# Macaron block with an S4 layer in the middle: waves of the quantized feed-forward regrouped, the last pair of a wave deferred, and a convolution with 28 block products

## The chip, the cores and the metric

The kernel runs on one core of one Trainium2 chip. The metric is the time of one execution on the device in microseconds (us). The engines are TensorE (PE, its weight loads listed apart as PEld), VectorE (DVE), ScalarE (ACT), GpSimd (POOL) and SyncE (SP), which here only issues transfers.

## The reference, cut to what matters

The input has 2 x 1024 rows of 1024 elements. Three stages are added to it, each on a layer norm of the running `x`:

```python
x = L0_attn_u                                      # (2, 1024, 1024)
x = x + 0.5 * ffn(layernorm(x))
x = x + s4(layernorm(x))
x = x + 0.5 * ffn(layernorm(x))                    # the same weights again

def ffn(x):                                        # 4-bit weights, groups of 128 rows
    Wg, Wu, Wd = (dequant(w) for w in (gate, up, down))   # (w4 - (z4 + 1)) * scale[group]
    return (silu(x @ Wg) * (x @ Wu)) @ Wd          # 1024 -> 2752 -> 1024

def s4(u):                                         # along the last axis, length L = 1024
    K = ifft(at_roots(Lambda, p, q, B, Ct, step)).real
    y = irfft(rfft(u, 2 * L) * rfft(K, 2 * L))[..., :L]   # a causal convolution with K
    return y + D * u
```

## The kernel before, in words

**Jobs.** The 2048 rows are cut into four blocks `b` of 512 rows (`TB`), of four tiles `t` of 128. A job `(b, k)` is one feed-forward on one block, first (`k` = 1) or second (`k` = 3). Eight jobs run in the order `(0,1) (1,1) (0,3) (1,3) (2,1) (3,1) (2,3) (3,3)`, here jobs 0 to 7. Each is `gate_up` and then `down`.

**gate_up.** The 2752 columns of gate and of up are 21 chunks `f` of 128 and a half chunk of 64. A *pair* is the gate and the up unit of one chunk; the half chunk's gate and up share one unit of 128. Each unit holds one of PSUM's eight banks as an accumulator `pg` (128 x 512). `WAVES` groups pairs into waves: five of three pairs, two of two, and one of two pairs and the half chunk. A wave has eight *steps*, one for each group of 128 input rows; `STEPS` has 64. A step multiplies every unit twice: with `hi` and `lo`, two parts of the transposed and normalized input (`xTh`, float32r; `xTl`, float16). The order in a step: the first half of the units with `lo`, then with `hi`; the other units with `hi`, then with `lo`. A unit's place in that list is its *position*: 0 is the first pair's gate, 1 its up, and so on.

**Rescales.** Quantized weights stay integers. After each group but the last, `scaled` multiplies the accumulator in place with the ratio of one group's scale to the next (L539 on ScalarE, L541 on VectorE); gate units go to ScalarE, up units to VectorE, and in job 0 position 1 also to ScalarE.

**gated.** When a pair has its eighth group, ScalarE makes `g` with Silu (L597), VectorE `hf` = up x `g` (L600), and GpSimd splits it into `hh` and `hl` (L602, L604). `hf` has two buffers (`hfpool`), `g` three. `gated_half` (L608 on) does the same for the half chunk with VectorE in GpSimd's place. Then `give_back` frees the pair's banks. `bank` hands out the bank that was handed out or given back longest ago and isn't held.

**down.** 2 x 22 steps: a half `a` of the output columns and a chunk `f`; four accumulators `po`, two matmuls each a step (`hl`, `hh`), rescaled in the same way.

**Weights.** `wq` and `wdq` are scratch in HBM with the integers as float32. Job 0 makes them while it runs (`first_weights`): the packed words are fetched, split into bytes (`split`), and `dequantize` subtracts the zero points on VectorE (L454 `q`, L486 `qd`) and writes to `wq` (L458) or `wdq` (L488) on SP. For wave `w` that is at steps 8w-12 to 8w-5; down's 48 pieces begin 12 steps before the end of `gate_up`, one a step, and go on in `down`. `load_w` (L523) and `load_down` (L531) read weights four steps ahead (`AHEAD`). Loads and dequantized tiles share one ring of buffers, `w` (`wpool`, 8).

**Hooks.** Other work is hung on steps by `at(up, step, ...)` for `gate_up` and `at(dn, step, ...)` for `down`; a hook is written ahead of its step's matmuls. After a first feed-forward the next job's `gate_up` carries the S4 stage of the previous block: `moments` and `deviations` (statistics), then for each of four tiles `norm` (VectorE), two steps on `swap` (`turn_whole`: eight transposes, a copy on ScalarE and one on VectorE), two steps on `conv`; then `moments` again and `save`, which writes the block to HBM. That is jobs 1, 2, 5 and 6. In jobs 2, 5 and 6 tile `t` has its `norm` at step 8 + 4t; in job 1 all is 30 steps later, since steps 2 on carry `s4_tables`, which makes the convolution kernel K (`s4_response`) and its Toeplitz matrix (`s4_toeplitz`) once. In jobs 3 and 4, step 44 has the statistics of the next block; in job 2 step 30 has a check of the group indices (`in_order`, `ps_ok`).

**convolve.** A tile's 1024 positions are eight blocks `c` of 128. The Toeplitz matrix has one 128 x 128 block per distance `d` (`blocks[:, d]`). The first four output blocks are ten block products (L915), the last four use sums and differences (`sums`, `after`, `ahead`), 21 blocks in 13 products (L934). In float32 the profile has two matmuls for each product. Three VectorE adds of 512 columns bring the results into `x` (L923, L950, L953).

**Order.** The calls above give the text an order, but a scheduler in the framework puts each engine's instructions into its queue; `in_order_of_writing` ties them to the text where it is used. Tiles of a pool get buffers from a ring by tag, and an instruction that needs a buffer waits until the last user is done.

Of the kernel before, what the change touches and what calls it, by code (L numbers as in the profile page):

```python
# [12 lines left out]
I32 = mybir.dt.int32  # L13
# [21 lines left out]
HALF = INTER - WIDE * P  # L35
WAVES = [list(range(3 * w, 3 * w + 3)) for w in range(5)] + [[15, 16], [17, 18], [19, 20]]
STEPS = [(w, g) for w in range(len(WAVES)) for g in range(GK)]
# [15 lines left out]
def macaron_s4_kernel(  # L53
# [40 lines left out]
    hpool = ctx.enter_context(tc.tile_pool(name="h", bufs=2 * NF))  # L94
    wpool = ctx.enter_context(tc.tile_pool(name="w", bufs=8))
    gpool = ctx.enter_context(tc.tile_pool(name="g", bufs=3))
# [28 lines left out]
    def t4(name):  # L125
        return xpool.tile([P, HID], F32, tag="x", name=name)
# [416 lines left out]
    def gate_up(j, b, hooks):  # L543
        hi, lo = pieces[b]
        ps = {}
        ready = {s: load_w(j, s) for s in range(AHEAD)}
        for s, (wi, g) in enumerate(STEPS):
# [15 lines left out]
            for k, pos, done in turns:  # L563
# [18 lines left out]
                if g < GK - 1:  # L582
                    on_act = unit % 2 == 0 or (j == 0 and pos == 1)
                    if unit == 2 * WIDE:
                        on_act = g % 2 == 0
                    scaled(on_act, p, p, rat[:, unit, g : g + 1])
                elif unit == 2 * WIDE:
                    gated_half(j, ps[unit])
                    give_back(ps.pop(unit))
                elif unit % 2:  # L590
                    gated(j, unit // 2, ps[unit - 1], ps[unit])
                    give_back(ps.pop(unit - 1), ps.pop(unit))
        pieces.pop(b)

    def gated(j, f, pg, pu):
        g = gpool.tile([P, TB], F32, tag="g", name=f"g_{j}_{f}")
        nc.scalar.activation(g, pg, AF.Silu, scale=rat[:, 2 * f, GK - 1 :])  # L597
        hf = hfpool.tile([P, TB], F32, tag="hf", name=f"hf_{j}_{f}")
        last = rat[:, 2 * f + 1, GK - 1 :]
        nc.vector.scalar_tensor_tensor(hf, pu, last, g, ALU.mult, ALU.mult)  # L600
        hi = hpool.tile([P, TB], F32R, tag="h", name=f"hh_{j}_{f}")
        nc.gpsimd.tensor_copy(hi, hf)  # L602
        lo = hpool.tile([P, TB], F32R, tag="h", name=f"hl_{j}_{f}")
        nc.gpsimd.tensor_tensor(lo, hf, hi.bitcast(F32), ALU.subtract)  # L604
        h[f] = (hi, lo)

# [57 lines left out]

    toeplitz = const.tile([P, HID], F32, tag="toeplitz", name="toeplitz")

    blocks = toeplitz.rearrange("p (d m) -> p d m", d=NC)
    after = const.tile([P, 3, P], F32, tag="after", name="after")
    ahead = const.tile([P, 3, P], F32, tag="ahead", name="ahead")
    k_dram = dpool.tile([1, P - 1 + HID], F32, tag="k", name="k_dram")  # L670
# [175 lines left out]
    def s4_response():  # L846

        tables = [t4("s4_tc"), t4("s4_ts")]
        for i in range(2):
            nc.sync.dma_start(tables[i], c_dft[:, i, :])  # L850
        ps = bank("s4_k")
        for r in range(8):
            for i in range(2):
                nc.tensor.matmul(  # L854
                    ps[:, r : r + 1],
                    tables[i].rearrange("p (a r) -> p r a", r=8)[:, r, :],
                    s4["se"][:, i, r : r + 1],
                    start=(i == 0),
                    stop=(i == 1),
                )  # L860
        k = t4("s4_response")
        d, none = k[:1, 8:9], k[:1, P : 2 * P - 1]
        nc.sync.dma_start(d, dskip.unsqueeze(0))
        nc.gpsimd.memset(none, 0.0)
        nc.vector.tensor_scalar(k[:, :8], ps[:, :8], 1.0 / HID, None, ALU.mult)
        nc.vector.tensor_tensor(k[:1, 0:1], k[:1, 0:1], d, ALU.add)
        nc.sync.dma_start(k_dram[:, : P - 1], none)
        nc.sync.dma_start(k_dram[0, P - 1 :].rearrange("(a r) -> a r", r=8), k[:, :8])
        s4.clear()

    def s4_toeplitz():

        both = [t4("s4_rows"), t4("s4_turn")]
        rows, turn = both[0], both[1][:, :P]
        nc.gpsimd.memset(turn, 0.0)
        nc.gpsimd.affine_select(
            out=turn,
            in_=turn,
            pattern=[[1, P]],
            compare_op=ALU.not_equal,  # L880
            fill=1.0,
            base=1 - P,
            channel_multiplier=1,
        )
        first = k_dram[:]
        nc.sync.dma_start(rows, bass.AP(first.tensor, first.offset, [[1, P], [1, HID]]))
        for i in range(NH):
            ps = bank(f"s4_t{i}")
            nc.tensor.matmul(ps, turn, rows[:, bass.ts(i, 512)], start=True, stop=True)
            dst = toeplitz[:, bass.ts(i, 512)]  # L890
            if i:
                nc.vector.tensor_copy(dst, ps)
            else:
                nc.scalar.copy(dst, ps)
        for dst, d in ((after, 3), (ahead, 1)):
            nc.vector.tensor_tensor(dst, blocks[:, d : d + 5 : 2], blocks[:, 2:7:2], ALU.subtract)

# [10 lines left out]
    def convolve(b, t, s, name):  # L908
# [3 lines left out]

        ps = bank(f"pc_{name}_0")
        for c in range(4):
            nc.tensor.matmul(  # L915
                ps[:, P * c :],
                s[:, c, :],
                toeplitz[:, : 512 - P * c],
                start=(c == 0),
                stop=(c == 3),  # L920
            )
        part = x[b][t][:, :512]
        nc.vector.tensor_tensor(part, part, ps, ALU.add)  # L923

        sums = ypool.tile([P, TB], F32, tag="y", name=f"sums_{name}")
        sums = sums[:, : 3 * P].rearrange("p (c t) -> p c t", c=3)
        nc.gpsimd.tensor_tensor(sums, s[:, 0:6:2, :], s[:, 1:6:2, :], ALU.add)
        own = bank(f"pc_{name}_1")
        both = bank(f"pc_{name}_2")[:, : 2 * P].rearrange("p (y m) -> p y m", y=2)
        flat = own.rearrange("p (y m) -> p y m", y=4)  # L930
        upper, lower = flat[:, 0:4:2], flat[:, 1:4:2]

        def product(dst, lhsT, rhs, start=False, stop=False):
            nc.tensor.matmul(dst, lhsT, rhs, start=start, stop=stop, skip_group_check=True)  # L934

        for y in range(2):
            product(flat[:, 2 * y : 2 * y + 2], s[:, 4 + 2 * y, :], blocks[:, 0:2], start=(y == 0))
        for y in range(2):
            product(flat[:, 2 * y + 1], s[:, 5 + 2 * y, :], blocks[:, 0])
        for i in range(3):  # L940
            y = slice(max(0, i - 1), 2)
            d = slice(max(0, 1 - i), 3 - i)
            product(lower[:, y], s[:, 2 * i, :], after[:, d])
            product(upper[:, y], s[:, 2 * i + 1, :], ahead[:, d], stop=(i == 2))
        for i in range(3):
            y = slice(max(0, i - 1), 2)
            d = slice(2 * max(1, 2 - i), 2 * (3 - i) + 1, 2)
            product(both[:, y], sums[:, i, :], blocks[:, d], start=(i == 0), stop=(i == 2))
        part = x[b][t][:, 512:]
        nc.vector.tensor_tensor(part, part, own, ALU.add)  # L950
        part = part.rearrange("p (y h m) -> p y h m", y=2, h=2)
        twice = both.unsqueeze(2).to_broadcast([P, 2, 2, P])
        nc.vector.tensor_tensor(part, part, twice, ALU.add)  # L953

# [14 lines left out]
    def general():  # L969
# [22 lines left out]
        def gather_table(dst, s_dram, z_dram, groups, n, name):  # L992
# [4 lines left out]
            for k in range(3):  # L997
                nc.sync.dma_start(s[32 * k : 32 * k + groups, :], s_dram)
            z = small.tile([P, P], I32, tag="z", name=f"z_{name}")[96:P, : n // 8]
            nc.gpsimd.memset(z, 0)  # L1000
# [162 lines left out]
        for b in range(TOK // TB):  # L1163
# [4 lines left out]
            for t in range(NT):  # L1168
                s = turn_whole(normalized(b, t), f"gt_{b}_{t}")
                convolve(b, t, s, f"g{b}_{t}")  # L1170
            feed_forward(b, 3)
# [9 lines left out]
    def fast():  # L1181
        for j, (b, k) in enumerate(JOBS):
# [7 lines left out]
            if prev:  # L1190
# [3 lines left out]
                if pk == 1:  # L1194
                    late = 30 if j == 1 else 0
                    at(up, 4, lambda: moments(pb, 2))
# [6 lines left out]
                    def swap(t):  # L1203
                        s4x[t] = turn_whole(s4n.pop(t), f"st_{pb}_{t}")

                    def conv(t):
                        convolve(pb, t, s4x.pop(t), f"{pb}_{t}")

                    for t in range(NT):
                        at(up, late + 8 + 4 * t, lambda t=t: norm(t))  # L1210
                        at(up, late + 10 + 4 * t, lambda t=t: swap(t))
                        at(up, late + 12 + 4 * t, lambda t=t: conv(t))
                    at(up, late + 27, lambda: moments(pb, 3))
                    at(up, late + 28, lambda: deviations(pb, 3, LIFT))

# [3 lines left out]

                    at(up, late + 28, save)  # L1220
                else:
# [196 lines left out]
```

## Time and profile before

| | us |
|---|---|
| median of 3 runs | 2207.82 (2206.94 to 2211.19) |
| the profiled execution's own time | 2209.4 |
| its span, first to last instruction | 2207.6 |
| TensorE busy | 2114.3 (96%) |
| VectorE busy | 1702.9 (77%) |
| ScalarE busy | 1428.7 (65%) |
| GpSimd busy | 368.1 (17%) |

The mean granted TensorE clock is 0.989 of full speed. A group of instructions is read as: line, engine, operation, what it writes from what it reads, shape, count, busy time, mean duration in ns, then the idle time before it and what ended most of it. A wait is read as: the waiting engine and line, what it waited for, us in total, times, longest. In the timeline a row has start and length in us, engine, line, tiles and count, and in brackets the idle time ahead of it. Durations of matmuls overlap, so TensorE's pace is read from starts.

### The profile page before, as it was taken

The page shows a single profiled execution, that of the slowest core. Times are in us where ns is not written, and L with a number is a line of the kernel's source. Part 1 is how long each engine was busy: PE and PEld are TensorE (multiplying, and loading weights), DVE is VectorE, ACT ScalarE, POOL GpSimd, SP SyncE. Part 2 cuts the span into 40 slices and gives each one's busy share as a digit, 9 for nine tenths or more (in the row PEclk, how much of TensorE's full clock was granted, in tenths as well). Part 3 has the DMA queues.
Part 4 walks back from the last instruction along what each step waited for, and adds up shares of the span by engine and source line. Part 5 has one row for each costly group of instructions (what it writes and reads, how often), then busy time and mean ns, then how long its engine had stood idle before and what let it go on. Part 6 is the DMA issues. An engine that isn't in the chain of part 4 may idle for free.

```text
span 2207.6 us, 28034 instructions
## 1 busy us (share of the span) xinstructions
PE 2114.3 (96%) x9524; PEld 1420.1 (64%) x9524; DVE 1702.9 (77%) x2803; ACT 1428.7 (65%) x2245; POOL 368.1 (17%) x389
## 2 busy tenths in 40 slices
PE   5888889999999999999999999999999999999998
PEld 3444565566877658755686558776587765865576
DVE  7777969777786877777877787867778677777776
ACT  5667777555764577666766667646676467766665
POOL 0223301222011230122102220112201122012310
PEclk9999999999999999999999999999999999999999
DMA  7768775434453545644655454534455354564443
GB/s 249 248 225 271 242 255 165 140 108 157 134 158 115 171 135 155 193 145 119 208 163 174 127 172 134 158 115 153 138 137 154 115 177 136 155 194 146 133 131 119
DMA packets 163669, 359.93 MB, mean 163 GB/s; under 512 B 22395, under 2 KB 27572, under 8 KB 163518
## 3 DMA queue, kind: packets, MB, share of 16 engines
q1 hardware_dynamic: 162670, 356.50, 52.1%
q8 instruction: 78, 1.28, 0.2%
q10 hardware_dynamic: 592, 1.16, 0.1%
q0 software_dynamic: 256, 0.39, 0.1%
q14 instruction: 73, 0.60, 0.1%
HBM read 306.86 MB, written 50.73 MB: 162 GB/s over the span
## 4 chain that ended last, share of the span: by engine, by line
PE 73%; issue 7%; DVE 5%; POOL 2%; ACT 1%; DVEq 0%; POOLq 0%; ACTq 0%
PE pg L572 42%; PE po L636 24%; PE pc L934 3%; PE pc L915 1%; POOL hl L604 1%; DVE pg L541 1%; PE pb L658 1%; PE pt L215 1%; DVE hf L600 1%; DVE po L541 1%; POOL hh L602 1%; PE st L215 1%; DVE qd L486 0%; PE s_k L854 0%; ACT g L597 0%
## 5 line engine op out<-in xcount | busy, mean ns | idle before, releaser
L539 ACT ACTIVATE pg<-pg,rat 128x512 f32<-128x512 f32 x1264 | 799.9, 661 | 489.3 <-PE pg L572 487.5
L541 DVE TENSOR_TENSOR pg<-pg,rat 128x512 f32<-128x512 f32 x1144 | 761.5, 694 | 180.9 <-PE pg L572 176.1
L572 PE MATMUL pg<-xTh,w 128*128 128x512 f32 x2752 | 874.2, 444 | 12.4 <-DVE pg L541 9.9
L572 PE MATMUL pg<-xTl,w 128*128 128x512 f16 x2752 | 737.8, 384 | 32.7 <-DVE pg L541 14.5
L572 PEld LDWEIGHTS pg<-xTh,w 128*128 128x128 f32 x2752 | 522.4, 190 | 192.6 <-DVE pg L541 24.3
L636 PE MATMUL po<-hl,wd 128*128 128x512 f32 x1344 | 540.5, 403 | 15.7 <-DMA wd<-wdq 7.5
L539 ACT ACTIVATE po<-po,ratd 128x512 f32<-128x512 f32 x670 | 438.1, 662 | 162.5 <-PE po L636 161.8
L636 PE MATMUL po<-hh,wd 128*128 128x512 f32 x1344 | 525.3, 392 | 0.0
L541 DVE TENSOR_TENSOR po<-po,ratd 128x512 f32<-128x512 f32 x610 | 420.9, 698 | 99.2 <-PE po L636 95.4
L572 PEld LDWEIGHTS <-w 128*128 128x128 bf16 x2752 | 227.8, 99 | 370.4 <-issue 186.1
L602 POOL CAST hh<-hf 128x512 fp32r<-128x512 f32 x168 | 109.4, 651 | 1530.7 <-DVE hf L600 976.1
L636 PEld LDWEIGHTS po<-hl,wd 128*128 128x128 f32 x1344 | 253.0, 188 | 92.1 <-DVE po L541 19.7
L636 PEld LDWEIGHTS po<-hh,wd 128*128 128x128 f32 x1344 | 253.6, 189 | 46.3
L604 POOL TENSOR_TENSOR hl<-hf,hh 128x512 fp32r<-128x512 f32 x168 | 222.9, 1327 | 13.4
L600 DVE SCALAR_TENSOR_TENSOR hf<-pg,rat,g 128x512 f32<-128x512 f32 x168 | 124.3, 749 | 90.6 <-ACT g L597 42.8
L597 ACT ACTIVATE g<-pg,rat 128x512 f32<-128x512 f32 x168 | 110.8, 687 | 48.7 <-PE pg L572 38.5
L178 DVE BATCH_NORM_STATS2 stats<-x 128x6 f32<-128x512 f32 x96 | 63.6, 677 | 1.1
L215 PE MATMUL pt<-ident,xn 128*128 128x128 f32 x256 | 42.6, 283 | 11.0 <-ACT xn L1286 11.0
L238 DVE TENSOR_TENSOR xTl<-pt,xTh 128x512 f16<-128x512 f32 x56 | 38.4, 690 | 14.2 <-ACT xTh L237 13.4
L660 DVE TENSOR_TENSOR x<-x,pb 128x512 f32<-128x512 f32 x64 | 43.2, 679 | 6.2 <-PE pb L658 6.0
L215 PEld LDWEIGHTS pt<-ident,xn 128*128 128x128 f32 x256 | 33.1, 145 | 21.8 <-ACT xn L1286 12.8
L237 ACT CAST xTh<-pt 128x512 fp32r<-128x512 f32 x56 | 33.0, 590 | 18.8 <-PE pt L215 18.6
(151 smaller groups left out, 816.9 us busy)
## 6 DMA issues: line engine op xcount, KB each, us to landing
w<-wq SPq DMA_DIRECT2D x319, 384.0 KB
wd<-wdq SPq DMA_DIRECT2D x336, 256.0 KB
w<-wq SPq DMA_DIRECT2D x128, 256.0 KB
w<-wq SPq DMA_DIRECT2D x64, 320.0 KB
x<-in_L_attn_u_dram SPq DMA_DIRECT2D x30, 512.0 KB
wq<-q SPq DMA_DIRECT2D x40, 384.0 KB
wdq<-qd SPq DMA_DIRECT2D x32, 256.0 KB
xs<-x SPq DMA_DIRECT2D x16, 512.0 KB
```

The lines of the kernel that those rows point to most:

```text
L178: nc.vector.bn_stats(stats[:, t, i, :], x[b][t][:, bass.ts(i, 512)])
L215: nc.tensor.transpose(ps[:, bass.ts(k, P)], n[:, bass.ts(k, P)], ident)
L539: nc.scalar.activation(dst, src, AF.Copy, scale=sc)
L541: nc.vector.tensor_tensor(dst, src, sc.to_broadcast([P, TB]), ALU.mult)
L572: nc.tensor.matmul(p, weights, (lo, hi)[k][:, g, :], start=(g == 0 and not done), stop=(g == GK - 1 and done), skip_group_check=True,)
L597: nc.scalar.activation(g, pg, AF.Silu, scale=rat[:, 2 * f, GK - 1 :])
L600: nc.vector.scalar_tensor_tensor(hf, pu, last, g, ALU.mult, ALU.mult)
L602: nc.gpsimd.tensor_copy(hi, hf)
L604: nc.gpsimd.tensor_tensor(lo, hf, hi.bitcast(F32), ALU.subtract)
L636: nc.tensor.matmul(ps[c], w[:, bass.ts(c, P)], part, start=(f == 0 and k == 0), stop=(f == NF - 1), skip_group_check=True,)
L660: nc.vector.tensor_tensor(part, part, ps, ALU.add)
L934: nc.tensor.matmul(dst, lhsT, rhs, start=start, stop=stop, skip_group_check=True)
```

## The change

`WAVES` becomes seven waves of three pairs; the half chunk joins the last one, which then has seven units and holds seven banks. `STEPS` has 56. The ring `w` gets 7 buffers, as wide as the new last wave (896 columns).

`gated` issues Silu at once and returns the rest (`hf`, `hh`, `hl`, `give_back`). For all pairs but a wave's last it is called immediately; the last pair's is called in the next wave's first step behind the rescale of position 1, or at the end of `gate_up`.

`convolve` is a generator with two parts, first and last four output blocks, the second one step later; it makes 28 blocks in 24 products, with more sums on GpSimd and five VectorE adds (512, 256 and three of 512 columns). Its hooks stand at `norm` 8 + 4t in jobs 2, 5 and 6, and 33 + 3t in job 1; the statistics after them come one step earlier in 2, 5 and 6, nine steps earlier in job 1.

`s4_response` computes K in one row and not in 8 columns on 128 partitions; `s4_toeplitz` keeps only the blocks and differences that are used.

```diff
-WAVES = [list(range(3 * w, 3 * w + 3)) for w in range(5)] + [[15, 16], [17, 18], [19, 20]]
+WAVES = [list(range(3 * w, 3 * w + 3)) for w in range(7)]
-    wpool = ctx.enter_context(tc.tile_pool(name="w", bufs=8))
+    wpool = ctx.enter_context(tc.tile_pool(name="w", bufs=7))
@@ def gate_up
+        waiting = []
+        def finish():
+            while waiting:
+                waiting.pop()()
...
                     scaled(on_act, p, p, rat[:, unit, g : g + 1])
+                    if pos == 1:
+                        finish()
...
-                    gated(j, unit // 2, ps[unit - 1], ps[unit])
-                    give_back(ps.pop(unit - 1), ps.pop(unit))
+                    rest = gated(j, unit // 2, ps.pop(unit - 1), ps.pop(unit))
+                    if unit // 2 == fs[-1]:
+                        waiting.append(rest)
+                    else:
+                        rest()
+        finish()
@@ def gated
         nc.scalar.activation(g, pg, AF.Silu, scale=rat[:, 2 * f, GK - 1 :])
+        def rest():
...
+            give_back(pg, pu)
+        return rest
@@ def s4_response
-        for r in range(8):
-            for i in range(2):
-                nc.tensor.matmul(ps[:, r : r + 1],
-                    tables[i].rearrange("p (a r) -> p r a", r=8)[:, r, :], s4["se"][:, i, r : r + 1], ...)
-        nc.vector.tensor_scalar(k[:, :8], ps[:, :8], 1.0 / HID, None, ALU.mult)
+        for half in range(2):
+            for r in range(4):
+                for i in range(2):
+                    nc.tensor.matmul(ps[:1, bass.ts(r, P)], s4["se"][:, i, 4 * half + r : 4 * half + r + 1],
+                        tables[i].rearrange("p (a r) -> p r a", r=8)[:, 4 * half + r, :], ...)
+            nc.vector.tensor_scalar(k[:1]..., ps[:1]..., 1.0 / HID, None, ALU.mult)
@@ def s4_toeplitz
+        nc.vector.tensor_copy(near[:, 0:3], blocks[:, 0:3])
+        nc.vector.tensor_copy(near[:, 3], blocks[:, 4])
         for dst, d in ((after, 3), (ahead, 1)):
-            nc.vector.tensor_tensor(dst, blocks[:, d : d + 5 : 2], blocks[:, 2:7:2], ALU.subtract)
+            own = dst[:, 0:3]
+            nc.vector.tensor_tensor(own, blocks[:, d : d + 5 : 2], blocks[:, 2:7:2], ALU.subtract)
+            nc.vector.tensor_tensor(dst[:, 3], dst[:, 2], dst[:, 1], ALU.subtract)
+            nc.vector.tensor_tensor(dst[:, 2], dst[:, 0], dst[:, 1], ALU.subtract)
+        for i in range(2):
+            nc.vector.tensor_tensor(middle[:, i], blocks[:, 2 + 4 * i], blocks[:, 4], ALU.subtract)
@@ def convolve, the new body
+        nc.gpsimd.tensor_tensor(sums[:, 0:3], s[:, 0:6:2, :], s[:, 1:6:2, :], ALU.add)
+        nc.gpsimd.tensor_tensor(quad, s[:, 0:2, :], s[:, 2:4, :], ALU.add)
+        nc.gpsimd.tensor_tensor(sums[:, 3], sums[:, 0], sums[:, 1], ALU.add)
+        for o in range(2):
+            if o:
+                yield
+            own = bank(f"pc_{name}_{o}")
+            flat = own.rearrange("p (d m) -> p d m", d=4)
+            mine = s[:, 4 * o : 4 * o + 4]
+            product(flat[:, 0:2], mine[:, 0], near[:, 0:2], start=True)
+            product(flat[:, 1], mine[:, 1], near[:, 0])
+            product(flat[:, 2:4], mine[:, 2], near[:, 0:2])
+            product(flat[:, 3], mine[:, 3], near[:, 0])
+            product(flat[:, 3], mine[:, 0], after[:, 0])
+            product(flat[:, 2], mine[:, 1], ahead[:, 0], stop=(o == 0))
+            both = bank(f"pb_{name}_{o}")
+            if o == 0:
+                product(both[:, :P], sums[:, 0], near[:, 2], start=True, stop=True)
+            else:
+                for y in range(2):
+                    product(flat[:, 2 * y + 1], s[:, 2 - 2 * y], after[:, 2 + y])
+                    product(flat[:, 2 * y], s[:, 3 - 2 * y], ahead[:, 2 + y], stop=(y == 1))
+                twice = both.rearrange("p (y m) -> p y m", y=4)
+                product(twice[:, 0], sums[:, 1], middle[:, 0], start=True)
+                product(twice[:, 1], sums[:, 0], middle[:, 1])
+                product(twice[:, 1], sums[:, 2], near[:, 2])
+                for y in range(2):
+                    product(twice[:, y], sums[:, 3], near[:, 3])
+                product(twice[:, 3], quad[:, 0], after[:, 1])
+                product(twice[:, 2], quad[:, 1], ahead[:, 1], stop=True)
...
@@ def fast, the S4 hooks
-                    late = 30 if j == 1 else 0
+                    o, gap = (33, 3) if j == 1 else (8, 4)
...
-                        at(up, late + 8 + 4 * t, lambda t=t: norm(t))
-                        at(up, late + 10 + 4 * t, lambda t=t: swap(t))
-                        at(up, late + 12 + 4 * t, lambda t=t: conv(t))
-                    at(up, late + 27, lambda: moments(pb, 3))
-                    at(up, late + 28, lambda: deviations(pb, 3, LIFT))
+                        s = o + gap * t
+                        at(up, s, lambda t=t: norm(t))
+                        at(up, s + 2, lambda t=t: swap(t))
+                        at(up, s + 4, lambda t=t: conv(t))
+                        at(up, s + 5, lambda t=t: next(parts[t], None))
+                    done = o + 3 * gap + 6
+                    at(up, done, lambda: moments(pb, 3))
+                    at(up, done + 1, lambda: deviations(pb, 3, LIFT))
...
```

## The prediction

> **What bounds the kernel now.** I read the page, then the chain of waits, VectorE's waits and its timeline at a wave boundary, then windows on the narrow waves of job 0.
>
> ```profile
> PE 2114.3 (96%) x9524; PEld 1420.1 (64%) x9524; DVE 1702.9 (77%) x2803; ACT 1428.7 (65%) x2245; POOL 368.1 (17%) x389
> ...
> 933.34 0.69 DVE pg L541
> 934.04 0.04 issue
> 934.08 21.32 PE pg L572 x94
> ...
> 955.41 0.70 DVE pg L541
> 956.11 0.04 issue
> 956.15 21.32 PE pg L572 x94
> ```
>
> TensorE is the bound: 96% busy, and the chain runs along it. It leaves it at one repeating place: a wave of three pairs is 21.3 us of matmuls, then a VectorE rescale of 0.7 us. TensorE's timeline shows a step of 12 matmuls every 2.695 us inside a wave (0.2246 us each), so eight steps want 21.56 us; waves come 22.05 us apart. Each boundary loses 0.49 us. VectorE's waits and timeline say why:
>
> ```profile
> DVE hf L600 <- POOL hl L604: 33.9, 29, 1.4
> ...
> 951.90 1.52 DVE L600 SCALAR_TENSOR_TENSOR hf<-pg,rat,g 128x512 f32<-128x512 f32 x2 [0.79 <-ACT g L597]
> 954.74 0.75 DVE L600 SCALAR_TENSOR_TENSOR hf<-pg,rat,g 128x512 f32<-128x512 f32 x1 [1.32 <-POOL hl L604]
> 955.41 2.53 DVE L541 TENSOR_TENSOR pg<-pg,rat 128x512 f32<-128x512 f32 x4
> ```
>
> The third pair's `hf` needs one of two `hf` buffers and waits 1.32 us for GpSimd (`hh` and `hl`, 0.61 + 1.30 us a pair). The next wave's first VectorE rescale is ready at about 954.0 and stands behind it until 955.41.
>
> A second loss is in the narrow waves 5 to 7 (208 matmuls, 46.7 us at the wide pace). By the timeline they take 48.4 us in jobs 2, 5, 6, 7, about 50.8 in jobs 3 and 4, where `moments` falls among them, and far more in job 0:
>
> ```profile
> 170.00:192.00 22.00, 16.36 (x72) 8.56 (x71) 15.73 (x26) 14.57 (x24) 7.49 (x8) 0.99 0.77 249
> 192.00:211.00 19.00, 17.14 (x65) 8.85 (x66) 13.99 (x19) 14.19 (x23) 4.87 (x4) 0.92 0.84 293
> 211.00:233.80 22.80, 19.27 (x80) 10.24 (x79) 16.98 (x28) 17.00 (x28) 5.66 (x6) 1.00 0.88 300
> ```
>
> Columns: length; busy time and count of PE, PEld, DVE, ACT, POOL; clock, DMA share, GB/s. No compute engine is full, the transfers nearly are (0.77 to 0.88), and TensorE's longest waits there are for `w<-wq`.
>
> [...] the rescale stood 1.4 us behind a waiting `hf`. [...] 333 ns a load in 32-byte steps (`s_k`), 190 ns packed.
>
> **The change, part by part.**
>
> *Convolution.* One tile runs from 1438.40 to 1445.13 in the timeline: 6.73 us for 31 blocks of 128 columns, two passes each. After, 28 blocks in 24 products: four of 256 columns (2 x 0.216) and twenty of 128 (2 x 0.1115, the spacing of the short ones), 1.73 + 4.46 = 6.19 us. Sixteen tiles: **-8.7 us**, straight on TensorE. VectorE gets a 256-wide and a 512-wide add more per tile (0.4 and 0.69 us), GpSimd sums of 256 and 128 columns (0.75 and 0.4 us, scaled from its 1.0 us for 384). Cover: waves 1 and 2 of job 5 are 36.8 us, TensorE full throughout, VectorE busy 25.6 and 24.9, GpSimd 13.1 and 7.6; two tiles add 2.2 and 2.3 us to each. I cost both at nothing; without cover up to 17 us. Part two enters a step later and takes two of eight banks while six are held; those of part one are by then a step old (2.7 us) and their adds take 1.1. In job 1 tiles come three steps apart and a transpose follows part two at once: 0 to +4, taken +1.
>
> *Deferred last pair.* Written order becomes rescale of position 1, then `hf`. If the queue follows: rescale at 954.05, `hf` at 954.75 without its wait, rescales of positions 3 and 5 done by 956.2 and 956.8, touched again at 956.8 and 957.2. No bubble; GpSimd's third pair isn't later, since it works on the second until 956.6. But the queue isn't always the text: `sums` stands two steps ahead of where it is written. Three boundaries (653, 1426, 1701 us) have the wanted order already, where `norm` made the first `hf` only 0.3 us later against the matmuls:
>
> ```profile
> 1428.03 0.70 DVE L541 TENSOR_TENSOR pg<-pg,rat 128x512 f32<-128x512 f32 x1 [0.44 <-PE pg L572]
> 1429.02 0.75 DVE L600 SCALAR_TENSOR_TENSOR hf<-pg,rat,g 128x512 f32<-128x512 f32 x1 [0.29 <-POOL hl L604]
> ```
>
> Matmuls ran on without a gap there. So the two are near a tie, and the new text leans the right way; I take it that they swap.
>
> *Seven waves and the deferral, jobs 1 to 7.* The 688 matmuls of a job stay, and the bytes of `w`: 56 loads, the last eight of 448 KB, for 64, never waited for after job 0. Time of each gate and up phase less its TensorE work at pace: 5.9 (job 1, wave 3 left out), 5.0, 6.3, 6.3, 2.5, 2.5, 3.9, sum 32.4 us. With no boundary bubble and no narrow wave I leave 0.6 a job (the first wave shows 0.3), 2.5 in job 2 for `ps_ok`, 1.0 in jobs 3 and 4 for `moments`, now among wide steps with a longer way from rescale to next touch, and 1.9 in job 1: 10.6. **-21.8 us.** If the order stays, 0.49 returns at six boundaries in jobs 3, 4, 7 and three in 1, 2, 5, 6 (convolution covers the rest): 14.7 left, -7.1.
>
> *Job 0.* Waves 5 to 7 take 64.2 us; 208 matmuls plus two losses of 6.3 (mean of waves 1 to 4 there: 4.3, 8.4, 8.6, 4.0) are 59.3: -4.9. Against it the ring `w` has 7 tiles, not 8. Five hold loads, so two, not three, are left for dequantized tiles. Adding up the SP queue's bytes in order of issue gives each write's landing; 13 us in all of the dequantizations after the start began before the write two earlier had landed. VectorE would wait so long, and rescales and the SP queue's next loads with it; with idle time on VectorE about a third counts, +4. Down's dequantizations move from step 52 to 44 with their loads, splits and writes on SP: same number, over longer steps, nothing. Sum -1, from -12 to +12.
>
> *Response and Toeplitz, once.* 32 passes at 0.238 us (7.6 us) become 32 passes of 128 columns in 32-byte steps, 0.11 to 0.238: 0 to -4, taken -2. VectorE gets two one-row copies of 512 and eight small block operations instead of two of 384, about +2.9 us; +1 of it shows. Convolution starts at step 37 instead of 42; the Toeplitz matmul stood at 446.4, 26 us ahead of the first product, so it still fits. `moments` and the four writes of `save` come nine steps earlier there. `save` holds SP until the convolution is done, 7.1 us at most by the waits of SP's own queue, and the loads of `w` behind it; the ring still runs six steps ahead, 16 us, so nothing is late.
>
> *Start of down.* `hf` and half compete for the two buffers: one VectorE operation (0.75 us) and one GpSimd pair more after the last matmul, in front of down's first rescales, while banks of the last pair come back later. Now it costs about 0.6 us a job; 0 to +0.8 more, taken 0.4: +3.
>
> *Sum.* -8.7 + 1 - 21.8 - 1 - 1 + 3 = -28.5. The profiled execution's span is 2207.6 and its own time 2209.4; the median of the runs shown, 2207.82, lies between. 2207.8 - 28.5 = **2179.3**.
>
> **The rivals.** *Order unchanged:* the deferral doesn't do what it says, because `hf` is queued as soon as it can be. For it: the order now is the same at 21 plain boundaries of jobs 2 to 7. Against: the tie. 14.7 us of the gain go: 2194. *Slower:* the ring of seven. If the loads, issued first, leave one tile and not two for dequantization, each waits for the one before: by the same sum 126 us after the start. For it: TensorE already waits for loads in job 0, and the share of DMA is 0.7 to 0.9. Against: the wait of VectorE on those landings is 1.5 us now, once. It decides from 23% of the tiles on (28.5 of 126); at 30%, +38 -28.5: 2217. *VectorE binds the convolution:* 16 x 1.1 us back with the order unchanged: 2211; 11 us of slack per wave speak against it.
>
> **How the numbers follow.** Forecast 0.47, with its own range 2168 to 2188; order unchanged 0.32 (2185 to 2203); slower 0.11; VectorE-bound or gains eaten 0.10. What a measurement can tell from no change is about 0.2%, 4.4 us. Range 2166 to 2206. Faster 0.82, same 0.07, slower 0.11.
>
> **What would show it.** Right: 28-block tiles of 6.2 us; VectorE's wait of `hf` on `hl` gone from 33.9 us; waves 21.6 us apart; job 0 near 202 us in gate and up (203.2 now). Wrong: three `hf` together at boundaries with 22.05 us kept; `q` on VectorE waiting for `wq` landings; waits for `pc` adds; a job 0 above 215 us.

## The result: no difference, and the profile after

| | before | after |
|---|---|---|
| median of 12 runs each, us | 2209.7 | 2211.72 (2205.83 to 2219.25) |
| profiled span, us | 2207.6 | 2211.5 |
| gate and up, jobs 1 to 7, us | 1262.7 | 1243.0 |
| down, jobs 1 to 7, us | 596.4 | 614.3 |
| job 0, gate and up / down, us | 204.5 / 103.8 | 207.6 / 106.9 |

The ratio is 1.0012, interval 0.9999 to 1.0025: no change that can be told, where 2179.3 was forecast. The phases are cut at TensorE's first matmul of each `gate_up` and `down` in the timeline; the last `down` ends with its last matmul. Gate and up became 19.7 us shorter and down 17.9 us longer. So a good part of the gain came, and was given back at another place.

From the page, the chain of waits and VectorE's waits and timeline of the kernel after, the same views that the prediction shows of the kernel before:

```profile
PE 2107.3 (95%) x9748; PEld 1432.8 (65%) x9748; DVE 1723.3 (78%) x2841; ACT 1418.3 (64%) x2238; POOL 387.1 (18%) x421
...
936.89 21.30 PE pg L578 x94
958.19 0.01 issue
958.20 0.70 DVE pg L541
958.90 0.04 issue
...
DVE hf L615 <- POOL hl L619: 49.7, 43, 1.4
...
954.70 1.53 DVE L615 SCALAR_TENSOR_TENSOR hf<-pg,rat,g 128x512 f32<-128x512 f32 x2 [0.79 <-ACT g L610]
957.53 0.75 DVE L615 SCALAR_TENSOR_TENSOR hf<-pg,rat,g 128x512 f32<-128x512 f32 x1 [1.31 <-POOL hl L619]
```

The boundary is as it was, which the prediction had named as a sign of being wrong: 21.3 us of matmuls, then a rescale on the chain. The third `hf` still waits 1.31 us for GpSimd, and the rescale still starts behind it, at 958.20. The deferral is in the text and not in VectorE's queue. Waves start 22.04 to 22.07 us apart, and the waits of `hf` on `hl` rose from 33.9 to 49.7 us: more waves end with three pairs, and the end of a job waits too.

The time was given back at the start of a job's `down`. This is VectorE there in job 5, before:

```profile
1593.11 0.75 DVE L600 SCALAR_TENSOR_TENSOR hf<-pg,rat,g 128x512 f32<-128x512 f32 x1 [0.34 <-ACT g L597]
1593.77 0.69 DVE L541 TENSOR_TENSOR po<-po,ratd 128x512 f32<-128x512 f32 x1
1594.85 0.76 DVE L614 SCALAR_TENSOR_TENSOR hf_half<-pg,rat,g_half 64x512 f32<-64x512 f32 x1 [0.39 <-POOL hl L604]
1595.64 0.70 DVE L541 TENSOR_TENSOR po<-po,ratd 128x512 f32<-128x512 f32 x1
...
1597.77 0.69 DVE L617 TENSOR_TENSOR hb<-hf_half,hb 64x512 fp32r<-64x512 f32 x1
```

This is VectorE at the same place after:

```profile
1596.47 0.76 DVE L632 SCALAR_TENSOR_TENSOR hf_half<-pg,rat,g_half 64x512 f32<-64x512 f32 x1 [1.09 <-POOL hl L619]
1598.38 0.75 DVE L615 SCALAR_TENSOR_TENSOR hf<-pg,rat,g 128x512 f32<-128x512 f32 x1 [1.16 <-POOL hl L619]
1599.17 0.42 DVE L634 CAST hb<-hf_half 64x512 fp32r<-64x512 f32 x1
1599.62 0.70 DVE L541 TENSOR_TENSOR po<-po,ratd 128x512 f32<-128x512 f32 x1
1600.35 1.62 DVE L635 TENSOR_TENSOR hb<-hf_half,hb 64x512 fp32r<-64x512 f32 x1
```

And this is the chain of waits that leads to the third pair's `hf`, in order of time (start, length, what):

```profile
1594.40 0.06 issue
1594.45 0.62 POOL hh L617
1595.08 0.07 issue
1595.14 1.29 POOL hl L619
1596.44 0.56 POOL hh L617
1597.00 0.07 issue
1597.07 1.29 POOL hl L619
1598.36 0.02 issue
1598.38 0.76 DVE hf L615
```

Before, down's first matmul was at 1592.37 and its first rescale on VectorE at 1593.77, 1.40 us later. After, the matmul was at 1594.72 and the rescale at 1599.62, 4.90 us later. In between the chain has left TensorE and runs through GpSimd's splits of two pairs. Here the deferral did reach the queue: the half chunk's `hf` stands ahead of the third pair's, each waits for a buffer that GpSimd must empty (1.09 and 1.16 us), and the rescales of `po` stand behind both. Then `hb` (L635, L617 before) takes 1.62 us, not 0.69.

TensorE's starvation there has a sequel in jobs 3 and 4. In these windows of job 3 (length; busy time and count of PE, PEld, DVE, ACT, POOL; clock, DMA share, GB/s) its clock falls just behind the gaps:

```profile
1074.00:1078.00 4.00, 2.19 (x10) 1.22 (x8) 3.75 (x5) 2.23 (x4) 2.17 (x3) 1.00 0.58 216
1078.00:1082.00 4.00, 3.50 (x10) 2.71 (x11) 2.99 (x5) 0.95 (x3) 0.00 (x0) 0.59 0.24 66
1082.00:1086.00 4.00, 4.00 (x19) 2.90 (x19) 2.91 (x5) 2.88 (x5) 0.00 (x0) 0.98 0.58 196
```

From 1078.5 on, matmuls of 512 columns start 427 ns apart and not 227, over seven intervals: 1.4 us more. Down of jobs 3 and 4 took 89.0 us, of jobs 1, 2, 5 and 6 87.3 to 87.5, against 85.4 to 85.5 before.

### The profile page after: what moved, and what is told of

Same layout as the page of the kernel before. It is cut to its first block, busy times and chain, and to the rows that moved or that the text cites. A ratio compares the mean times of both kernels' runs of the same rounds, so it can differ in the third digit from the quotient of the medians.

```text
span 2211.5 us, 28423 instructions
## 1 busy us (share of the span) xinstructions
PE 2107.3 (95%) x9748; PEld 1432.8 (65%) x9748; DVE 1723.3 (78%) x2841; ACT 1418.3 (64%) x2238; POOL 387.1 (18%) x421
## 3 DMA queue, kind: packets, MB, share of 16 engines
q10 hardware_dynamic: 592, 1.16, 0.1%
## 4 chain that ended last, share of the span: by engine, by line
PE 83%; DVE 9%; DMA 3%; issue 1%; POOL 1%; ACT 1%; SPq 0%; DVEq 0%; ACTq 0%; POOLq 0%
PE pg L578 49%; PE po L654 26%; PE pc L956 3%; DVE pg L541 3%; PE pb L956 1%; PE pb L676 1%; DVE q L454 1%; DVE hf L615 1%; DMA w<-wq 1%; POOL hl L619 1%; PE pt L215 1%; DVE stats L178 1%; PE st L215 1%; DMA wdq<-qd 1%; DVE po L541 1%
## 5 line engine op out<-in xcount | busy, mean ns | idle before, releaser
L539 ACT ACTIVATE pg<-pg,rat 128x512 f32<-128x512 f32 x1257 | 790.6, 660 | 466.3 <-PE pg L578 462.7
L578 PE MATMUL pg<-xTh,w 128*128 128x512 f32 x2752 | 841.9, 435 | 15.4 <-DVE pg L541 11.9
L578 PE MATMUL pg<-xTl,w 128*128 128x512 f16 x2752 | 718.0, 383 | 27.1 <-DMA w<-wq 17.3
L617 POOL CAST hh<-hf 128x512 fp32r<-128x512 f32 x168 | 108.9, 648 | 1506.3 <-DVE hf L615 792.0
L615 DVE SCALAR_TENSOR_TENSOR hf<-pg,rat,g 128x512 f32<-128x512 f32 x168 | 124.4, 749 | 88.0 <-POOL hl L619 49.7
L956 PEld LDWEIGHTS pc<-near,st 128*128 128x128 f32 x256 | 43.7, 191 | 7.8
```

The costliest lines, as they stand in the source:

```text
L539: nc.scalar.activation(dst, src, AF.Copy, scale=sc)
L578: nc.tensor.matmul(p, weights, (lo, hi)[k][:, g, :], start=(g == 0 and not done), stop=(g == GK - 1 and done), skip_group_check=True,)
```

## The experiments

For each kernel the table has the median; the ratio to before, run beside it (medians 2208.4 to 2209.7), with its 95% interval; jobs 1 to 7 of the profiled execution by phase; and the *rest*, which is the median less those two sums: job 0, the start and the end. Jobs 1 to 7 vary little from execution to execution, so the rest shows job 0 better than one profile does: e8 and e10, which have the same jobs 1 to 7, agree there within 0.2 us, though e10's profiled execution took 9.4 us more than its median. Where the clock falls in some jobs the agreement is worse: after and e9, again with the same jobs, differ by 2.7 us. Each kernel has one profile and 4 to 21 runs, and the intervals of the ratios are 3 to 10 us wide; so a difference of under some 5 us between two variants can't be told from none by the medians.

| kernel | median | ratio | gate and up 1 to 7 | down 1 to 7 | rest |
|---|---|---|---|---|---|
| before (69 runs) | 2209.0 | 1 | 1262.7 | 596.4 | 349.8 |
| after | 2211.7 | 1.0012 [0.9999, 1.0025] | 1243.0 | 614.3 | 354.4 |
| e1 no deferral | 2190.4 | 0.9923 [0.9906, 0.9939] | 1241.6 | 603.0 | 345.8 |
| e2 deferral tied | 2190.2 | 0.9920 [0.9897, 0.9943] | 1230.8 | 612.5 | 346.8 |
| e3 three `hf` buffers | 2192.1 | 0.9929 [0.9913, 0.9946] | 1229.7 | 604.5 | 357.9 |
| e4 convolution alone | 2197.8 | 0.9948 [0.9932, 0.9965] | 1250.5 | 596.4 | 350.9 |
| e5 ring of 7 alone | 2212.2 | 1.0019 [1.0012, 1.0027] | 1264.3 | 596.1 | 351.9 |
| e6 last wave at once | 2202.3 | 0.9965 [0.9954, 0.9977] | 1242.4 | 602.9 | 357.0 |
| e7 tied, last wave at once | 2180.3 | 0.9863 [0.9847, 0.9878] | 1230.7 | 603.2 | 346.3 |
| e8 three `hf`, last wave at once | 2190.0 | 0.9912 [0.9899, 0.9926] | 1229.6 | 602.4 | 357.9 |
| e9 job 0 at once | 2204.3 | 0.9977 [0.9967, 0.9986] | 1243.5 | 616.5 | 344.3 |
| e10 as e8, job 0 at once | 2183.2 | 0.9874 [0.9856, 0.9892] | 1229.7 | 602.2 | 351.4 |
| e11 as e7, half chunk late | 2173.1 | 0.9834 [0.9818, 0.9850] | 1230.5 | 597.1 | 345.5 |
| e12 all | 2170.3 | 0.9822 [0.9808, 0.9837] | 1230.3 | 592.3 | 347.8 |

The theory was that the boundaries keep their order and the deferral costs time at the start of down; the rivals, that the waves or the ring cost it, or that job 0 does.

**e1, every pair at once.**

```diff
-                    if unit // 2 == fs[-1]:
-                        waiting.append(rest)
-                    else:
-                        rest()
+                    rest()
```

> The kernel after, with every pair's rest() called at once. Theory (order at the start of down): the deferral hangs the last pair of the last wave behind the half chunk, so two VectorE operations that wait for GpSimd stand ahead of the first rescale of down; undone, that rescale goes ahead of the half chunk again and each job gets back 1 to 2 of the 1.9 to 3.6 us that its down has gained: 8 to 14 us under the kernel after, so 2198 to 2204. Rival (banks: with seven of eight held, down waits for the last pair's banks): the banks come back no sooner, no change beyond 2 us. Second rival (the deferral helped at the wave boundaries and this hid in the sum): the boundaries lose time again and the kernel gets slower than the one after.

Without the deferral the kernel is 21.3 us faster than after (2190.4 against 2211.7). Gate and up of jobs 1 to 7 hardly move (1.4 us): at the boundaries the deferral did nothing. Down gives 11.3 us, the rest 8.6. The sum is more than the 8 to 14 us that were expected, since nothing was expected of job 0. So the gain of the rest of the change, 18.7 us, was lost to the deferral.

**e2, the deferred pair tied behind the rescale of position 1 in VectorE's queue.**

```diff
-                        finish()
+                        in_order_of_writing(finish, ET.DVE)
```

> The kernel after, with the deferred rest tied on VectorE behind the rescale of position 1. Theory (the text's order never reached VectorE's queue at plain boundaries): the 0.49 us bubbles of about 22 boundaries go, 9 to 12 us under the kernel after, and nothing changes in down: 2199 to 2203. Rival (order of these two does not matter, GpSimd's pace does): waves stay 22.05 us apart, no change.

This is VectorE at the same boundary of job 3 in e2's timeline:

```profile
942.29 1.53 DVE L615 SCALAR_TENSOR_TENSOR hf<-pg,rat,g 128x512 f32<-128x512 f32 x2 [0.79 <-ACT g L610]
944.45 0.70 DVE L541 TENSOR_TENSOR pg<-pg,rat 128x512 f32<-128x512 f32 x1 [0.63 <-PE pg L578]
945.12 0.75 DVE L615 SCALAR_TENSOR_TENSOR hf<-pg,rat,g 128x512 f32<-128x512 f32 x1
```

This is the order that the prediction wrote down: rescale, then `hf`, without a wait. Waves come 21.57 us apart, 0.01 over TensorE's pace, and gate and up are 12.2 us shorter than after. The price of a boundary and its cause were right; the text alone did not bring the order about, the tie did. The median fell by 21.5 us, twice what was expected: another 7.6 us of it stands in the rest, so the tie changes job 0 too.

**e3, three `hf` buffers** (and 43 in the ring of `h` for 44, to make room).

```diff
-    hpool = ctx.enter_context(tc.tile_pool(name="h", bufs=2 * NF))
+    hpool = ctx.enter_context(tc.tile_pool(name="h", bufs=2 * NF - 1))
-    hfpool = ctx.enter_context(tc.tile_pool(name="hf", bufs=2))
+    hfpool = ctx.enter_context(tc.tile_pool(name="hf", bufs=3))
```

> The kernel after with three hf buffers (and 43 instead of 44 h buffers, to make room). Theory (two hf buffers are behind both losses): no wait of hf on hl is left, boundaries lose nothing (-11 us) and down starts without the stall of 2.7 us, in jobs 3 and 4 without the slow clock after it (-18 to -24 us in all eight jobs): 2178 to 2186. Rival (order): the half chunk and the last pair still stand ahead of down's first rescales, only without waiting; down gets back less than half, 2190 to 2196. Rival (banks): down unchanged, 2199 to 2202.

The boundaries lose 0.01 us here too, and down falls to 86.5 us in jobs 1 to 6. Both losses are waits for one of two buffers. The rest is 357.9, so the total is no better than e2's, and the 2178 to 2186 of the theory was missed by some 6 us.

**e4, the convolution alone:** the waves, the ring and `gated` of before with the new `convolve`, `s4_response`, `s4_toeplitz` and hooks.

```diff
-WAVES = [list(range(3 * w, 3 * w + 3)) for w in range(7)]
+WAVES = [list(range(3 * w, 3 * w + 3)) for w in range(5)] + [[15, 16], [17, 18], [19, 20]]
-    wpool = ctx.enter_context(tc.tile_pool(name="w", bufs=7))
+    wpool = ctx.enter_context(tc.tile_pool(name="w", bufs=8))
-                    if unit // 2 == fs[-1]:
-                        waiting.append(rest)
-                    else:
-                        rest()
+                    rest()
```

> The convolution, response and Toeplitz of the kernel after, with the old eight waves, 8 w buffers and no deferral. Theory: 0.43 to 0.54 us a tile on TensorE, 7 to 9 us, and about 2 us of the response: 2198 to 2202 against 2209.7 before. Rival (VectorE's added operations eat it): within 3 us of before.

The kernel is 11.3 us faster than before. Waves 1 to 3 of job 5 went from 95.17 to 93.00 us, 0.54 a tile. With e1 this splits the change: convolution -11.3, waves and ring -7.4, deferral +21.3. With four runs of e1 and of e4 the -7.4 is uncertain by some 5 us or more.

**e5, the ring of seven alone.**

```diff
-    wpool = ctx.enter_context(tc.tile_pool(name="w", bufs=8))
+    wpool = ctx.enter_context(tc.tile_pool(name="w", bufs=7))
```

> The kernel before with a ring w of 7 buffers instead of 8 and nothing else. My prediction's step: +4 us, all in job 0 (2213.7 against 2209.7). Rival 'slower' (each dequantized tile waits for the one before from 30% of the tiles on): +38 us, and waits of q or qd on VectorE for their landings of over 20 us. No effect: 2209.7 +- 2, with the gate and up phase of job 0 between 203 and 206 us.

The ratio, 1.0019, is 4.2 us of 2209; the forecast was 4. It is not 38: the rival of the ring is out. By the sums 1.3 us of it stand in job 1 and 2.1 in the rest.

**e6, the deferral in waves 0 to 5 only.**

```diff
-                    if unit // 2 == fs[-1]:
+                    if unit // 2 == fs[-1] and wi < len(WAVES) - 1:
```

> The changed kernel with the deferral in waves 0 to 5 only; the last wave's pair is finished at once, so that the half chunk stands behind it. Theory A (the deferral costs only where it ends a job, at the start of down): as without any deferral, 2190 +- 4, down of jobs 1 to 7 at 86.4 us each, plain wave boundaries still 0.48 us. Rival B (holding the third pair's banks and its split into the next wave costs job 0 too, which took 13.6 us longer in the profile with the deferral than without): only the 12.5 us of jobs 1 to 7 come back, 2199, and gate and up of job 0 stays above 204 us.

Down of jobs 1 to 7 gets back the 11.4 us, and the rest does not come back: 357.0. Theory A fell; rival B was nearer (2199 expected, 2202 measured). So the deferral has two costs, one at the start of down and one in job 0.

**e7, both places mended:** e6 with the tie of e2, and, a third change, the half chunk's `hf` from the ring of `h`.

```diff
-                        finish()
+                        in_order_of_writing(finish, ET.DVE)
-        hf = hfpool.tile([P, TB], F32, tag="hf", name=f"hf_{j}_half")
+        hf = hpool.tile([P, TB], F32, tag="h", name=f"hf_{j}_half")
```

> As the run before, with the deferred pair in waves 0 to 5 tied behind the rescale of position 1 on VectorE, and the half chunk's hf taken from the ring of h, so that it doesn't wait for GpSimd. Theory A: both losses go, 30 boundaries of jobs 1 to 7 without convolution at 0.01 instead of 0.48 us, down at 86 us: 2190 - 11 (what tying gave before, less job 0) = 2179. Rival: the boundaries' gain is taken back at the next place, 2186 or more.

The median is 2180.3, near the 2179 of theory A. The boundaries lose 0.01 us, and the rest is 346.3. Down stays at 86.4 to 86.5 us in jobs 1 to 5: the other buffer for the half chunk brought nothing. Its wait of 0.55 us (e6, job 5) went, and no wait of `hf_half` is left in e7's list of waits; what took the time instead was not shown.

**e8, e6 with three `hf` buffers** (the two lines of e3).

> The changed kernel with three hf buffers (43 in the ring of h) and the deferral in waves 0 to 5 only. Theory A: boundaries at 0.01 us without a tie, and at the end of a job four hf operations without a wait for GpSimd ahead of down's first rescale: down of jobs 1 to 7 at 85.5 us, 2192 (three hf buffers with the deferral everywhere) - 7 = 2185 if job 0 stays at 208 us in gate and up, 2175 if it is at 197. Rival: the start of down is bound by GpSimd's split, not by the buffers: down stays at 86.5 us.

Down stays at 86.3, so the rival was right there: it isn't the buffer. What it is shows in VectorE's timeline at the start of down:

```profile
1579.08 0.76 DVE L632 SCALAR_TENSOR_TENSOR hf_half<-pg,rat,g_half 64x512 f32<-64x512 f32 x1 [0.26 <-POOL hl L619]
1579.87 0.70 DVE L541 TENSOR_TENSOR po<-po,ratd 128x512 f32<-128x512 f32 x1
1580.60 0.65 DVE L634 CAST hb<-hf_half 64x512 fp32r<-64x512 f32 x1
1581.28 0.70 DVE L541 TENSOR_TENSOR po<-po,ratd 128x512 f32<-128x512 f32 x1
1582.01 1.62 DVE L635 TENSOR_TENSOR hb<-hf_half,hb 64x512 fp32r<-64x512 f32 x1
1583.66 1.30 DVE L541 TENSOR_TENSOR po<-po,ratd 128x512 f32<-128x512 f32 x2
```

Only 0.26 us of waiting is left, but the half chunk's three operations (3.0 us) stand ahead of and between the rescales, and `hb` takes 1.62 us, as in the kernel after, where GpSimd makes the third pair's `hl` in 1.07 us of that time (job 5). That they set the length of `down` is tested in e11.

**e9, job 0 without the deferral.**

```diff
-                    if unit // 2 == fs[-1]:
+                    if unit // 2 == fs[-1] and j > 0:
```

> The changed kernel with the deferral in jobs 1 to 7 only. Theory B (in job 0 the untied deferral costs time, since VectorE's and TensorE's queues are then put together differently among the dequantizations): what is left of the median after taking off jobs 1 to 7 of the profile is 346 to 351 us, as without deferral, and not 354 to 358 as in the four kernels with an untied one; 2211.7 - 8 = 2203.5, the start of down still at its loss. Rival (job 0 is a matter of chance from kernel to kernel): 2211 +- 3.

It takes 7.5 us less than after, with a rest of 344.3: that the deferral in job 0 costs time is shown, though not that the order of the queues is why. Its down is even longer than after's, since four jobs, not two, are at 88.7 to 89.0. In job 3, one of them, TensorE was busy for 2.53 of the 4 us from 1064 on, at a granted clock of 1.00; in the next two stretches of 4 us the clock was 0.65 and 0.93.

**e10, e8 with job 0 at once** (the line of e6 with `and j > 0`).

> Three hf buffers, deferral in waves 0 to 5 of jobs 1 to 7 only. Theory B: jobs 1 to 7 stay at 1832 us by the profile, the rest falls from 358 to 346 to 351, 2178 to 2183. Rival (chance, or the 43 buffers of h cost job 0): 2190.

It takes 6.7 us less than e8, in the same direction, but not clear of chance: its four runs lie from 2178.9 to 2192.6, e8's five from 2186.9 to 2191.8. The rest, 351.4, is just above what was expected. Whether the 43 buffers of `h` or the third `hf` buffer cost something in job 0 was not tested alone.

**e11, e7 with the half chunk's VectorE work in `down`:** the three operations become a function that `gated_half` returns, called behind down's third step, and `hf` comes from its own two buffers again. The line that calls it:

```diff
+            if d == 2:
+                in_order_of_writing(late.pop(), ET.DVE)
```

> The kernel with the deferred pair tied, the last wave's pair at once, and the half chunk's VectorE work (hf, hb, hb) moved behind down's third step, two hf buffers. Theory: the half chunk is what delays down's first rescales by its three operations, one of them slowed beside GpSimd; down of jobs 1 to 7 falls from 86.4 to 85.4 us as in the kernel before, -7 us against the version with the half chunk at its place, 2173. Rival: hf of the third pair still waits for GpSimd (1.1 us) ahead of the first rescale and sets the start; down at 86 or more, 2178 to 2181.

The median is 2173.1 for an expected 2173; down falls to 85.4 to 85.5 in jobs 1 to 6, the length before the change, though three pairs and not two end the last wave. The third pair's `hf` still waits 1.08 us ahead of the first rescale (job 5), so it was the half chunk's operations, and not that wait, that had put down above its length before the change.

**e12, all in one:** e10 with the half chunk late.

> All in one: three hf buffers, deferral in waves 0 to 5 of jobs 1 to 7, the half chunk's VectorE work behind down's third step. Theories together: jobs 1 to 7 at 1832 - 7 = 1825 us or less by the profile, the rest at 346 to 351: 2171 to 2176. Rival: the start of down doesn't gain and job 0 stays at 358: 2190.

The median is 2170.3, 38 us below the kernel before and the lowest median here, though its runs (2168.9 to 2172.6) overlap with e11's (2169.2 to 2175.9). This is VectorE at the start of down:

```profile
1563.72 1.65 DVE L614 SCALAR_TENSOR_TENSOR hf<-pg,rat,g 128x512 f32<-128x512 f32 x2 [0.18 <-PE pg L578]
1565.29 1.53 DVE L541 TENSOR_TENSOR po<-po,ratd 128x512 f32<-128x512 f32 x2
```

Down's first matmul is at 1563.88, its first two rescales follow at 1565.29 without a wait, and down takes 84.8 us, 0.7 less than in e11, where `hf` waits.

## Why the prediction was wrong, step by step

The forecast was -28.5 us. The median after is 2.7 above the 69 runs before, which is no change that can be told. Of the 31 us between, some 11 are in gate and up of jobs 1 to 7 (forecast -30.5, measured -19.7), 15 in down (+3, measured +17.9) and 6 in job 0 (-1, measured +4.6 in the rest).

**Deferred last pair: the step that failed first.** "I take it that they swap." They didn't. The forecast priced the swap at 14.7 us; the unchanged order left that out, and tying it (e2) brought 12.2. With the tie, waves and deferral bring 19.7 us in gate and up (e4 to e2) where 21.8 was forecast. Three boundaries that had the wanted order were read as a sign of a near tie, which the text would tip. The text did not. Why the scheduler left `hf` ahead is open; that it did is shown by the timeline. The rival "order unchanged" described this, and its 2194 is near e1's 2190.4, the change without the deferral; it is not near the 2211.7 of the change itself, since the deferral did harm that the rival did not name.

**Start of down: the term mis-sized most.** It was put at 0.4 us a job, 0 to 0.8. Measured: 1.8 to 3.6 a job (2.6 on average over jobs 1 to 7), in two parts. Three pairs at the end of the last wave, without a deferral, cost 0.95 a job (e4 to e1, 6.6 us). The deferral there costs 1.6 a job more (e1 to after, 11.3 us), by the waits of two `hf` operations for GpSimd, both ahead of down's first rescale, and in jobs 3 and 4 by the lower clock. The step saw that `hf` and the half chunk compete for two buffers in front of down's first rescale, and put that at 0.4 us; it did not add up the waits. Two operations wait there, 1.09 and 1.16 us, and the first rescale came 4.90 us after the first matmul and not 1.40. It says nothing of `hb`, which takes longer there: `hb<-hf_half,hb` took 0.69 us in all eight jobs before, never beside an `hl`, and 1.61 to 1.62 in all eight jobs after, with 1.06 to 1.08 us of an `hl` in that time. Why it takes longer was not shown.

**The clock.** No step had it. In job 3 after, the trace has the slower pace, 427 ns for 227, and ahead of it two pauses of 1.6 and 1.1 us over the pace, with matmuls between. Nearly the same pauses in job 5 left the clock at 1.00. What differs is where they fall. In the clock records of the traces before and after, the drops are to 0.50 and last 3.41 us or a multiple of it (but for the one that runs into the end). In each trace every drop starts a whole number of times 3.413 us behind the first (after, the first is at 92.26, and those of jobs 3, 4 and 7 at 1078.71, 1327.88 and 2119.78: 289, 362 and 594 times). The time from the first drop on is therefore cut here into stretches of this length. These are two of job 3 and two of job 5 after, in the columns of the windows above:

```profile
1075.30:1078.71 3.41, 1.75 (x7) 1.21 (x8) 3.32 (x5) 0.97 (x2) 1.79 (x2) 1.00 0.41 162
1078.71:1082.12 3.41, 3.41 (x10) 2.62 (x10) 2.28 (x4) 1.05 (x2) 0.00 (x0) 0.50 0.28 77
1597.53:1600.95 3.42, 1.93 (x11) 1.26 (x11) 2.47 (x4) 2.30 (x4) 2.49 (x3) 1.00 0.25 77
1600.95:1604.36 3.41, 2.58 (x12) 1.85 (x11) 3.38 (x5) 1.26 (x2) 0.47 (x1) 1.00 0.00 0
```

In job 3 the second pause and a part of the first fall into one stretch, and TensorE is busy for 1.75 of its 3.41 us (0.51); in job 5 the pauses fall into two (0.56 and 0.76). The drops of jobs 4 and 7 after stand behind stretches with a busy share of 0.45 and 0.50. All other stretches of jobs 1 to 7, counted from 340 us on, have 0.56 or more after and 0.62 or more before, in each case up to the last matmul of `down`. So in these two traces it is the share of one stretch that goes with the drop, and which jobs are hit depends on how the pauses lie to the stretches. Where the limit lies, and whether other kernels keep to it, was not shown. One drop does not fit: in job 1 before, at 434.02 for 6.83 us, it follows one-column matmuls of `s4_response`, in stretches that are fully busy by the view (3.41 of 3.41 us).

**Job 0.** The terms were -4.9 for the waves and +4 for the ring. The ring was right (e5: +4.2, partly in job 1), the waves perhaps better than forecast: e4 to e1 takes 5.1 off the rest, with the ring's price in it, which is about the size of the uncertainty. The deferral wasn't expected to matter there and costs 8.6 (e1 to after), shown from the other side by e9 (7.5 in the median) and, less surely, by e10. TensorE's time over pace in waves 5 and 6 of job 0 is 6.9 to 9.4 us in the four kernels without it in job 0 (e1, e9, e10, e12), and 15.1 to 18.7 in the seven with it. Where it is tied (e2, e7, e11) waves 2 to 4 lose 16 us instead of 21 to 30, and the rest is as without it. In TensorE's queue of the built programs the last unit of wave 5 falls five steps behind its neighbours where job 0 defers, and two where it does not. That this is the cause was not tried, and it is not all: the tied kernels have it too.

**Convolution.** Right in size: 0.54 us a tile was forecast, 0.54 measured in e4, and 0.44 in the whole change (93.43 us for the same three waves). VectorE and GpSimd covered it, and the rival that VectorE binds it is out. With response and Toeplitz matrix -8.7 was forecast and -11.3 measured; the rest is in job 1 (4.2 us less gate and up) and in a boundary of job 5 that lost 0.58 us and loses none now.

**Seven waves with the order unchanged.** Forecast -7.1 in gate and up of jobs 1 to 7, +3 in down and -1 in job 0, so -5.1; measured -7.4 (e4 to e1), by other shares: -8.9 in gate and up, +6.6 in down, -5.1 in the rest. That the sums are close is in part luck.

So two steps failed: the order that the text was to bring about, and the price of the deferral where it hides behind nothing, at the start of down, with a cost in job 0 for which the forecast has no term. The convolution, the price of a boundary and the ring were right. e7, which makes the assumed order true and takes the deferral away from the last wave, gives 2180.3. That this is within 1 us of the forecast 2179.3 is luck in part: against before, gate and up is at -32.0 (forecast -30.5), down at +6.8 (+3) and the rest at -3.5 (-1).

## What to carry to other kernels

A deferral in the text is a wish: see in the timeline whether the queue has the order, and tie it if it hasn't. The same edit must be looked at where the loop ends, since the deferred work there has nothing left to hide behind and stands ahead of the next phase's first step. Where operations stand behind a waiting one on their engine, as the rescale behind the third `hf` here (1.31 us), count not only the operations added but which waiting one stands first in the queue.

## What was not expected of the hardware

- Pauses of TensorE of under 2 us each were followed by a granted clock of 0.50 for 3.41 us, 1.4 us on top of the pauses (job 3, after), where TensorE was busy for 0.51 of the 3.41 us ahead of the drop. Nearly the same pauses spread over two such stretches (0.56 and 0.76; job 5, after) left the clock at 1.00.
- The VectorE subtraction of 64 x 512 (`hb<-hf_half,hb`) took 0.69 us without GpSimd's `hl` beside it (before) and 1.62 with it (after), about as much longer as they overlap (1.07 us). The cast `hb<-hf_half` took 0.42 without an `hl` (after), 0.63 to 0.64 with 0.35 to 0.36 us of one (before, jobs 1 to 7) and 1.35 with 1.07 (before, job 0). The rescales in PSUM stayed at 0.70 or under beside it (before).
- The rest moves from 344 to 358 us from kernel to kernel, though the deferral adds no work to job 0 and takes none away.
